# A graph network on one core: the degree sort issued beside most of the normalisation, 21 blocks gathered in the first layer, 18 gathered and 31 multiplied in the last

## The chip, the cores and the metric

The kernel runs on one core of a Trainium2 chip. The metric is the device time of one execution in microseconds (us), the median of several. Five engines work side by side, each through a queue of its own, in order: TensorE (PE in the profile, with its weight loads as PEld), VectorE (DVE), ScalarE (ACT), GpSimd (POOL) and SyncE (SP), which issues most of the plain DMAs. Indirect DMAs (gathers and scatters by a list of row numbers) are issued by POOL.

## The reference

```python
h = jnp.maximum(_layernorm(x, axis=-1), 0.0)          # x: 6250 nodes x 256
def agg(h):                                           # src, dst: 100000 edges
    return jax.ops.segment_sum(h[src], dst, num_segments=6250)
x_ = h
for l in range(3):
    h = x_ + agg(x_)
    h = relu(h @ W1s[l] + b1s[l])
    h = relu(h @ W2s[l] + b2s[l])
    x_ = h @ W3s[l] + b3s[l]
h = x_ + agg(x_)
h = relu(h @ cW1 + cb1)
h = relu(h @ cW2 + cb2)                               # 256 -> 64
out = x + (h @ cW3 + cb3)                             # 64 -> 256
```

There are four layers: three of the loop (numbered 0 to 2) and the head (3). The edges come sorted by destination. The heavy part is `x_ + agg(x_)`, a product with a sparse matrix of 6250 x 6250 counts.

## The kernel before, in words

The 6250 nodes are 49 tiles of 128 rows (`NT`). The first 36 tiles' worth of nodes (`NS`) are sorted by in-degree into 36 "s" blocks of 128 nodes, block 0 having the lowest degrees; the other 13 tiles stay as they are ("u" blocks). In each layer every block is done in one of two ways.

- *Multiplied.* The block's counts (how many edges go from each source node to each of its nodes) are built once, in layer 0, as a matrix of bytes by `build` (lines 1285 to 1341), and stored in DRAM (`mats`). In every layer they are loaded again, turned into floats by ACT (line 2118) and multiplied on PE with all the nodes' features, held in SBUF as two halves, a rounded one and the rest (`XY`). Line 2154 does that: for a panel of 3 or 4 blocks, 49 tiles x 4 matmuls of 384 or 512 columns, 196 matmuls in all. A panel is an entry `(first, number)` of `early` (layer 0), `wide` (layers 1 and 2) or `final` (layer 3), which count along the list of slots `seq`.
- *Gathered.* For each of the block's 128 nodes the c-th edge's source row is fetched by one indirect DMA of 128 rows (line 1830), two of them into one buffer, and DVE adds them up (lines 1866 to 1888). A block takes as many gathers as its cap, the highest in-degree that `reach` allows for it from the binomial law, and in layer 0 one more for the nodes' own rows. The caps of blocks 0 to 20 are 9, 10, 11, 12, 12, 12, 13, 13, 14, 14, 14, 14, 15, 15, 15, 16, 16, 16, 16, 17, 17. `nodes_of` names the gathered blocks of each layer.

Before the change layer 0 multiplies 29 blocks and gathers 20, layers 1 and 2 multiply 28 and gather 21, layer 3 multiplies 30 and gathers 19; the counts of 30 blocks are built. In gathers that is 294, 291, 291 and 257. All three small matrix products that follow (`mlp`, lines 1604 to 1750) are the same for both kinds. Results of "s" blocks are put back in their places by one indirect DMA per block from POOL (`place_rows`, lines 596 to 607).

The order on every engine is written out by hand: Python generators (`normed`, `look`, `ranking`, `listed`, `build`, `stored_later`) issue a piece of work at each `next()`, and the sequence of the calls is the order in the queues.

- `normed` (line 1022) loads x, normalises it in 25 pairs of tiles, multiplies it by the first weight and fills `XY`. After the three calls that start it, it yields 60 times, twice for each step s = 0 to 29. In step s it loads, scales pair s on ACT (1064), turns pair s-1 on PE and ACT, multiplies pair s-2 on PE (1085), copies pair s-3 out of PSUM (`out`, 1093), rounds pair s-4 on ACT (`high`, 1097), subtracts (`low`, 1102), stores pair s-5, and takes the moments of later pairs on DVE (1044).
- `look` (line 708, 24 yields) finds where each group of four nodes begins among the sorted edges: a gather of nearby edges, 17 counts on DVE (803) and ACT (807), then 16 gathers of edges by POOL (`ask`, 702), whose results DVE and ACT split and PE turns in four quarters (845 to 861). From them come the codes of the u blocks (`clT`) and of the s nodes (`cN`).
- `ranking` (line 910) counts each node's degree from `cN` and ranks the nodes (944 to 1015, PE, ACT and DVE in turn); its result is `goal`. Its last part scatters one row for each of the 36 blocks to `ranks` in DRAM (line 1017, issued at 603 by POOL).
- `listed` (line 1922) loads `ranks` back (`got`, 1925), fetches the edges of the blocks to be gathered (1931), and makes the lists of row numbers for line 1830 with DVE. On its 11th call DVE copies the node numbers out of `got` (1965); on its 14th the first list is made and layer 0's gathers begin.

Between the normalisation and layer 0's products, 28 units (`PRE`) of the counts are built, eight to a block. Then `product` (line 2126) goes tile by tile; in its layer-0 form it also calls `build` after a plan (`goals`) and `listed` at every second tile of panel 0, at every third after it. The gathers are paced over a layer by a clock of planned PE time (`work_of`, `ByNode.flow`), and each waits for the matmul issued last when it was planned (`after`).

Lines 1138 to 1203 hold the order around the change. Calling the 60 yields of `normed` h = 0 to 59: the first pieces of `look` come at h = 0 to 17, its 4 quarters at h = 25 to 41, its end after h = 51; `ranking` comes at h = 17 (its constants) and at h = 42 to 50; its 36 scatters come after h = 59, all at once. `listed` is first called in tile 0 of panel 0.

Of the kernel before, what the change touches and what calls it, by code (L numbers as in the profile page):

```python
# [9 lines left out]
F32 = mybir.dt.float32  # L10
# [6 lines left out]
OP = mybir.AluOpType  # L17
PSUM = bass.MemoryType.PSUM
DRAM = bass.MemoryType.DRAM
P = 128  # L20
# [400 lines left out]
def sorted_edges(  # L421
# [93 lines left out]
    lists_of = nodes_of[0] + [(20, 1)]  # L515
    assert sum(n for _, n in lists_of) == max(KS)
    for b0, n in lists_of:
        for b in range(b0, b0 + n):
# [17 lines left out]
    begins = const.tile([P, NS], F32, name="begins")  # L536
# [59 lines left out]
    def place_rows(key, ap, b, sb, at=None, **kw):  # L596

        at = ids if at is None else at

        if placing[0]:  # L600
            nc.gpsimd.memset(mark, 0.0)
        placing[0] = True
        got = nc.gpsimd.indirect_dma_start(  # L603
            out=ap, out_offset=bass.IndirectOffsetOnAxis(ap=at[:, b:b + 1], axis=0),
            in_=sb, in_offset=None, **kw)
        wrote(key, got, True)
# [303 lines left out]
    def ranking(pool):  # L910
# [9 lines left out]
        yield  # L920
        lag = pool.tile([P, P], F32, name="rel", bufs=1)
        nc.gpsimd.iota(lag, pattern=[[1, P]], base=0, channel_multiplier=-GD,
                       allow_small_or_imprecise_dtypes=True)
        SUB = P // GD
        row = pool.tile([P, 2], F32, name="row", bufs=1)
        nc.vector.memset(row[:, 0:1], 0.0)
        for t in range(1, GD):
            nc.vector.tensor_scalar(row[:, 1:2], place, float(SUB * t), float(P - 1), op0=OP.is_ge,
                                    op1=OP.mult)
            nc.vector.tensor_tensor(row[:, 0:1], row[:, 0:1], row[:, 1:2], OP.add)  # L930
        nc.vector.tensor_scalar(row[:, 1:2], row[:, 0:1], 0.0, None, op0=OP.is_gt)
        less_t = pool.tile([P, 2, P], BF16, name="less_t", bufs=1)
        nc.vector.tensor_scalar(less_t[:SUB, 1], lag[:SUB], float(GD - 1), -1.0, op0=OP.is_equal,
                                op1=OP.mult)
        nc.vector.tensor_scalar(lag, lag, row[:, 0:1], None, op0=OP.add)
        this = pool.tile([P, P], F32, name="f", bufs=1)
        nc.vector.tensor_scalar(this, lag, 0.0, None, op0=OP.is_equal)
        nc.vector.tensor_scalar(lag, lag, -1.0, row[:, 1:2], op0=OP.is_equal, op1=OP.mult)
        nc.vector.tensor_tensor(less_t[:, 0], this, lag, OP.subtract)
# [77 lines left out]
        yield  # L1017
        for g in range(NS):
            place_rows("ranks", ranks[:, :], g, what[:, g, :], goal)


    def normed(pool, ps_t, ps_z):
# [75 lines left out]

        def low(s):
            i0, n = pairs[s]  # L1100
            engine = nc.vector if EASY[0] <= s < EASY[1] else nc.gpsimd
            engine.tensor_tensor(XY[:, i0:i0 + n, C:], zs[s][:, :n, :],
                                    XY[:, i0:i0 + n, :C].bitcast(F32), OP.subtract)

# [31 lines left out]
            yield  # L1136

    sums = ps_g.tile([P, W], F32, name="sums")
    LOOK = (25, 27, 30, 32, 34, 36, 39, 41, 51, 53)
    RANK = tuple(range(42, 51))  # L1140
    LATER = (20, 30)

    with tc.manual_schedule():
        with tc.tile_pool(name="norm", bufs=2) as norm, tc.tile_pool(
            name="prep", bufs=2
        ) as prep, tc.tile_pool(
            name="ps_t", bufs=2, space=PSUM
        ) as ps_t, tc.tile_pool(name="ps_z", bufs=2, space=PSUM) as ps_z:
            cN = prep.tile([P, 2 * NS, GSUB], BF16, name="cN", bufs=1)
            looked = look(prep)  # L1150
            ranked = ranking(prep)
            next(looked)
            rows = normed(norm, ps_t, ps_z)
            next(rows)
# [8 lines left out]
            next(rows)  # L1163
            next(looked)
            for t, pattern, base in ((cols[:, :U * TWO], [[1, U], [2 * STEP, TWO]], NS),
                                     (cols[:, U * TWO:], [[1, NS], [2 * STEP, TWO]], 0),
                                     (lanes, [[1, P]], 0), (colf, [[1, P]], 0)):
                nc.gpsimd.iota(t, pattern=pattern, base=base, channel_multiplier=0,
                               allow_small_or_imprecise_dtypes=True)
            next(rows)  # L1170
            next(rows)
            next(looked)
            next(rows)
            turn_biases()
            nc.vector.tensor_copy(ident_r, ident)
            next(looked)
            next(rows)
            next(rows)
            for k in range(2 * NLAYER):
                next(looked)  # L1180
                next(rows)
                next(rows)
            next(looked)
            next(ranked)
            next(ranked)
            stores = stored_later(prep)
            for h, _ in enumerate(rows, 18):
                if h % 2:
                    ask(2)
                if h in LOOK:  # L1190
                    next(looked)
                if h in RANK:
                    next(ranked)
                if h in LATER:
                    next(stores)
            next(looked)
            next(ranked, None)
            assert next(ranked, 0) == 0 and next(looked, 0) == 0 and next(stores, 0) == 0

        work = ctx.enter_context(tc.tile_pool(name="work", bufs=1))  # L1200
        mat = {}
# [572 lines left out]
        class ByNode:  # L1774
# [36 lines left out]

            def send(self, upto, early=False):
                if self.l == 0:
                    upto = min(upto, self.upto[min(self.listed, len(self.upto)) - 1])
# [353 lines left out]
        def yields(slots):  # L2168
            return UNITS * slots + (slots > TOP)
# [2 lines left out]
        built, goals = [0], []  # L2172
        u0, g0 = 0, UNITS * FIRST + EARLY
        for p in range(last[0] + 1):
            u1, g1 = p * NT + NT - 2 * CH - 3, total if p == last[0] else yields(
                sum(n for _, n in early[:p + 2]))
# [7 lines left out]
        with tc.tile_pool(name="hots", bufs=1) as hots, tc.tile_pool(  # L2184
# [11 lines left out]
            while now[0] < PRE:  # L2196
                next(beside)
                next(ahead_w, None)
                built[0] += 1
                tick(layers[0])  # L2200
                layers[0].advance()
                if built[0] == UNITS * (FIRST - 1) + 3:
                    at = chunks.tile([P, 4, CH * P], U8, name="at", bufs=5)
                    nc.sync.dma_start(out=at[:, :FIRST - 1, :], in_=mats[0][:, :FIRST - 1, :CH * P])
                if built[0] == UNITS * FIRST:
                    mat[0, 0] = [(at[:, :FIRST - 1, j * P:(j + 1) * P], own_at[0][:, j, :])
                                 for j in range(CH)]
                    for _ in range(2):
                        fetch(0, 0)
# [81 lines left out]
```

## Time and profile before

| | |
|---|---|
| time, 3 runs | 1942.61 us median (1937.9 to 1942.84) |
| the profiled execution | 1944.59 us, of which the span 1942.8 us |
| mean granted PE clock | 0.977 |
| PE busy | 1814.7 us (93%), 8982 matmuls |
| POOL busy | 1396.8 us (72%) |
| ACT busy, DVE busy | 1182.1 us (61%), 898.7 us (46%) |
| product with the counts (line 2154) | 5880 matmuls, 1427.6 us |
| gathers (line 1830) | 1133, 1092.8 us |

The stages by the first and last instructions on PE: normalisation to 130.5 us, the first units of counts to 159.5, layer 0 to 673.6, layer 1 to 1098, layer 2 to 1561, layer 3 to the end. A busy share is read within its stage: POOL's instructions for indirect DMAs have some 0.3 us between them in which the profile shows no work and no wait, so that POOL at 75% is a POOL that issues without a pause.

### The profile page before, as it was taken

What the parts mean: (1) busy time and instruction counts of PE and PEld (TensorE: products, weight loads), DVE (VectorE), ACT (ScalarE), POOL (GpSimd) and SP (SyncE); (2) the same over time, 40 slices, a digit from 0 to 9 for tenths busy, and PEclk for the clock granted to TensorE, in tenths of its full rate; (3) what the DMA queues carried; (4) which work ended last, traced back from release to release, by engine and by line L of the source; (5) the groups of instructions that cost most, each with busy time, mean ns of one, the idle gap of its engine ahead of it and who ended that gap; (6) DMA issues with size and microseconds to landing.
All of it is one profiled execution on the core that took longest, in us unless ns stands there. A gap on an engine that the chain in (4) does not pass through costs nothing. (4 is left out here: it accounts for less than half of the span.)

```text
span 1942.8 us, 28380 instructions
## 1 busy us (share of the span) xinstructions
PE 1814.7 (93%) x8982; PEld 1404.6 (72%) x8982; DVE 898.7 (46%) x1892; ACT 1182.1 (61%) x2259; POOL 1396.8 (72%) x1604
## 2 busy tenths in 40 slices
PE   5777989999999989999998999999998999999896
PEld 3556777776777767777776767777776677778784
DVE  6666688777764253232334353333334343332332
ACT  4646667676766576556655475555664576666562
POOL 3557777777777577677777777777777776777775
PEclk9878999999999999999999999999999999999898
DMA  6434556666666596566565675656555776666564
GB/s 183 128 96 150 166 182 206 193 196 219 197 199 187 172 297 208 159 186 201 181 193 174 217 237 173 182 161 189 180 176 169 234 219 191 158 181 151 154 180 85
DMA packets 244986, 355.11 MB, mean 183 GB/s; under 512 B 34248, under 2 KB 199512, under 8 KB 244506
## 3 DMA queue, kind: packets, MB, share of 16 engines
q0 software_dynamic: 67792, 169.41, 30.6%
q1 hardware_dynamic: 176504, 182.73, 29.9%
q8 instruction: 72, 1.18, 0.3%
q10 hardware_dynamic: 530, 1.07, 0.2%
q14 instruction: 88, 0.72, 0.1%
HBM read 286.82 MB, written 71.78 MB: 185 GB/s over the span
## 5 line engine op out<-in xcount | busy, mean ns | idle before, releaser
L2154 PE MATMUL agg<-a,XY 128*128 128x512 f32 (+1 forms) x5880 | 1427.6, 395 | 17.8 <-ACT a L2118 14.8
L1830 POOL DMA_INDIRECT rows<-table,idxN x1113 | 1072.9, 964 | 381.2 <-PE agg L2154 162.9
L2154 PEld LDWEIGHTS agg<-a,XY 128*128 128x128 f32 x5880 | 1078.2, 190 | 246.6 <-ACT a L2118 28.5
L2118 ACT CAST a<-at 128x512 fp32r<-128x512 uint8 (+1 forms) x1463 | 846.8, 604 | 319.1 <-PE agg L2154 313.6
L1870 DVE TENSOR_TENSOR sums<-sums,rows 128x512 f32<-128x512 f32 x467 | 325.7, 697 | 552.3 <-DMA rows<-table,idxN 541.6
L1318 ACT CAST at<-bp 128x392 uint16<-128x392 f32 x213 | 103.8, 490 | 111.5 <-PE bp L1310 107.6
L1731 PE MATMUL ps<-w,h 128*128 128x256 f32 x576 | 133.5, 385 | 0.4 <-ACT h L1635 0.4
L1632 PE MATMUL ps<-h,w 128*128 128x512 f32 (+1 forms) x296 | 129.9, 581 | 3.0 <-DVE xt L1736 3.0
L1731 PEld LDWEIGHTS ps<-w,h 128*128 128x128 f32 x576 | 111.0, 193 | 17.9 <-ACT h L1635 1.1
L1256 DVE TENSOR_TENSOR lo<-lanes,pairs 128x512 bf16<-128x512 bf16 x240 | 99.7, 422 | 31.6 <-PE bp L1310 30.5
L1310 PE MATMUL bp<-hi,lo 128*128 128x98 bf16 x964 | 87.3, 215 | 24.3 <-DVE lo L1256 21.0
L1310 PEld LDWEIGHTS <-lo 128*128 128x128 bf16 x964 | 53.6, 101 | 76.0 <-DVE lo L1256 35.7
L603 POOL DMA_INDIRECT table<-zz,ids x92 | 90.7, 986 | 24.0 <-issue 16.2
L1632 PEld LDWEIGHTS ps<-h,w 128*128 128x128 f32 x296 | 55.8, 189 | 57.3 <-issue 43.9
L1736 DVE TENSOR_TENSOR zz<-ps,w 128x512 f32<-128x512 f32 x66 | 43.7, 672 | 107.5 <-PE ps L1731 105.9
L1905 ACT ACTIVATE h<-pt,bias 128x256 f32<-128x256 f32 (+1 forms) x80 | 33.1, 466 | 93.4 <-PE pt L1897 93.4
L1635 ACT ACTIVATE h<-ps,bias 128x512 f32<-128x512 f32 (+1 forms) x74 | 48.8, 678 | 50.0 <-PE ps L1632 50.0
L1256 DVE TENSOR_TENSOR hi<-hi,pairs 128x784 bf16<-128x784 bf16 x120 | 68.2, 568 | 4.2
L1866 DVE COPY sums<-rows 128x512 f32<-128x512 f32 x61 | 42.3, 694 | 57.4 <-DMA rows<-table,idxN 56.6
L603 POOL DMA_INDIRECT out_dram<-zz,ids x36 | 57.1, 1587 | 15.2 <-issue 8.5
L1256 DVE TENSOR_TENSOR hi<-cols,pairs 128x784 bf16<-128x784 bf16 x120 | 67.5, 562 | 0.9 <-ACT pairs L1244 0.9
L1416 DVE TENSOR_TENSOR XY<-turned,XY 128x512 fp32r<-128x512 f32 x54 | 37.3, 695 | 65.3 <-ACT XY L1420 65.0
(253 smaller groups left out, 987.3 us busy)
## 6 DMA issues: line engine op xcount, KB each, us to landing
at<-mat SPq DMA_DIRECT2D x126, 448.0 KB
mat<-at SPq DMA_DIRECT2D x30, 784.0 KB
at<-mat SPq DMA_DIRECT2D x62, 336.0 KB
rows<-table,idxN POOLq DMA_INDIRECT x1113
turned<-table SPq DMA_DIRECT2D x54, 256.0 KB
at<-mat SPq DMA_DIRECT2D x70, 112.0 KB
u<-own SPq DMA_DIRECT2D x61, 128.0 KB
own<-zz SPq DMA_DIRECT2D x53, 128.0 KB
```

The source lines that it names most:

```text
L603: got = nc.gpsimd.indirect_dma_start(out=ap, out_offset=bass.IndirectOffsetOnAxis(ap=at[:, b:b + 1], axis=0), in_=sb, in_offset=None, **kw)
L1256: nc.vector.tensor_tensor(o, values, which[:, :, None, :].to_broadcast(shape), op)
L1310: mm = nc.tensor.matmul(bp[:, m * HW:(m + 1) * HW], lo[:, m, :], hi[:, m, :], start=(i == 0), stop=(i == len(sets) - 1))
L1318: nc.scalar.copy(o, v)
L1632: mm = nc.tensor.matmul(ps[:, :w], weights[l][0][:, c, i * P:(i + 1) * P], h1[:, c, :w], start=(c == 0), stop=(c == KC - 1))
L1635: later(soon, lambda: nc.scalar.activation(h2[0][:, i, :w], ps[:, :w], AF.Relu, bias=b2[l][:, i:i + 1]))
L1731: mm = nc.tensor.matmul(o, h2[0][:, c, nodes], w3[:, c, :], start=(c == 0), stop=(c == KC - 1))
L1736: later(soon, lambda: nc.vector.tensor_tensor(z[:, :m, :], v, w3[:, KC:, :].to_broadcast([P, m, C]), OP.add))
L1830: got = nc.gpsimd.indirect_dma_start(out=t[:, c % 2, :], out_offset=None, in_=tables[self.l][:, :], in_offset=bass.IndirectOffsetOnAxis(ap ...
L1870: nc.vector.tensor_tensor(sums, sums, rows.rearrange("p h c -> p (h c)"), OP.add)
L2118: nc.scalar.copy(o, v)
L2154: mm = nc.tensor.matmul(agg[c][:, :w], XY[:, j, o:o + P], a[:, :w], start=(i == 0 and half == 0), stop=(i == NT - 1 and half == 1))
```

## The change

The kernel after differs in four things.

1. *Blocks.* Layer 0 gathers 21 blocks and multiplies 28 (panels of 3, 3, 3, 3, 4, 4, 4, 4 blocks in place of 3, 3, 3, 4, 4, 4, 4, 4); layer 3 gathers 18 and multiplies 31 (one panel of 3 becomes one of 4). Counts are built for 31 blocks. In gathers: 312, 291, 291 and 241. Layers 1 and 2 stay as they are.
2. *Order beside the normalisation.* The pieces of `look` and `ranking` are put at other yields t of `normed`: the counts at t = 7 and 8 all together, the 16 asks at t = 8 to 13, the four quarters at t = 12 to 21, the ranking at t = 22 to 30, and the scatters to `ranks` one at each t from 31 to 59, the last seven beside the first units of the counts. The stores of padding and of a copy of `src` move from h = 30 to t = 16, the end of `look` to t = 33 to 39.
3. *Engines.* The constants of `ranking` (`row`, `lag`, `less_t`) are made by POOL, not DVE, at t = 3. `out` is on ACT for the pairs 2 to 15 (14 pairs; before, 9 odd ones from 7 on), else on DVE. `low` is on POOL for pairs 6 to 16 (11 pairs; before, 20), else on DVE (14; before, 5).
4. *Lists.* `listed` is called in the last 10 of the 28 units ahead of layer 0, once the scatters have been issued, so that its 14th call comes at tile 6 of panel 0 (before, tile 26) and its 11th at tile 0 (before, tile 20).

```diff
-        ("u", b) for b in range(NT - 4, NT)] + [("s", 19)]
-    early = [(0, 3), (3, 3), (6, 3)] + [(b, 4) for b in range(9, 29, 4)]
+        ("u", b) for b in range(NT - 4, NT)] + [("s", 19), ("s", 18)]
+    early = [(b, 3) for b in range(0, 12, 3)] + [(b, 4) for b in range(12, 24, 4)] + [(25, 4)]
-    final = [(b, 4) for b in range(4, 24, 4)] + [(24, 3), (27, 3), (0, 4)]
+    final = [(b, 4) for b in range(4, 28, 4)] + [(28, 3), (0, 4)]
-    nodes_of = [[(16, 4), (12, 4), (8, 4), (4, 4), (1, 3), (0, 1)]] + [
+    nodes_of = [[(17, 4), (13, 4), (9, 4), (5, 4), (1, 4), (0, 1)]] + [
-        [(15, 4), (11, 4), (7, 4), (3, 4), (1, 2), (0, 1)]]
+        [(14, 4), (10, 4), (6, 4), (2, 4), (1, 1), (0, 1)]]
-    DEG, LOW, EASY = 28, 7, (9, 14)
+    DEG, LOW, EASY = 28, 7, (6, 17)
...
-        nc.vector.memset(row[:, 0:1], 0.0)
+        nc.gpsimd.memset(row[:, 0:1], 0.0)
...
         for g in range(NS):
             place_rows("ranks", ranks[:, :], g, what[:, g, :], goal)
+            yield
...
-            copy = nc.scalar.copy if s > 5 and s % 2 else nc.vector.tensor_copy
+            copy = nc.scalar.copy if 2 <= s < 16 else nc.vector.tensor_copy
...
-            engine = nc.vector if EASY[0] <= s < EASY[1] else nc.gpsimd
+            engine = nc.gpsimd if EASY[0] <= s < EASY[1] else nc.vector
...
-    LOOK = (25, 27, 30, 32, 34, 36, 39, 41, 51, 53)
-    RANK = tuple(range(42, 51))
-    LATER = (20, 30)
+    L, R, S = "look", "rank", "store"
+    BESIDE = {0: (L, "lanes"), 2: (L,), 3: ("turn", L, R), 7: (L, L), 8: (L,) * 5, 9: (4,), 11: (4,),
+              12: (L,), 13: (4, L), 14: (S,), 15: (L,), 16: (L, S), 17: (L,), 18: (L,), 20: (L,), 21: (L,),
+              33: (R, L), 36: (R, L), 39: (R, L)}
+    BESIDE.update({t: (R,) for t in range(22, 60) if t not in BESIDE})
...
-        EARLY = 4
+        EARLY, LISTED = 4, 18
...
             while now[0] < PRE:
                 next(beside)
                 next(ahead_w, None)
+                if next(ranked, 0) == 0 and built[0] >= LISTED:
+                    next(lists)
                 built[0] += 1
```

A number in `BESIDE` is a call of `ask` for so many edge gathers.

More of the change, by code (lines that the diff above doesn't have):

```diff
@@ L514, in sorted_edges @@
     starts_of, wide_of, end_of = {}, {}, 0
-    lists_of = nodes_of[0] + [(20, 1)]
+    lists_of = nodes_of[0]
     assert sum(n for _, n in lists_of) == max(KS)
@@ L535, in sorted_edges @@
     clT = const.tile([P, 3, GSUB, 2 * BUILT], BF16, name="clT")
-    begins = const.tile([P, NS], F32, name="begins")
     place = const.tile([P, 1], F32, name="place")
@@ L1149, in sorted_edges @@
             cN = prep.tile([P, 2 * NS, GSUB], BF16, name="cN", bufs=1)
+            begins = prep.tile([P, NS], F32, name="begins", bufs=1)
             looked = look(prep)
@@ L1153, in sorted_edges @@
             rows = normed(norm, ps_t, ps_z)
+            stores = stored_later(prep)
             next(rows)
@@ L1162, in sorted_edges @@
             next(rows)
[L1163 to L1195, printed above, removed]
@@ L1196, in sorted_edges @@
-            next(looked)
-            next(ranked, None)
-            assert next(ranked, 0) == 0 and next(looked, 0) == 0 and next(stores, 0) == 0
+            for t, _ in enumerate(rows):
+                for one in BESIDE.get(t, ()):
+                    if one == "lanes":
+                        for to, pattern, base in (
+                                (cols[:, :U * TWO], [[1, U], [2 * STEP, TWO]], NS),
+                                (cols[:, U * TWO:], [[1, NS], [2 * STEP, TWO]], 0),
+                                (lanes, [[1, P]], 0), (colf, [[1, P]], 0)):
+                            nc.gpsimd.iota(to, pattern=pattern, base=base, channel_multiplier=0,
+                                           allow_small_or_imprecise_dtypes=True)
+                    elif one == "turn":
+                        turn_biases()
+                        nc.vector.tensor_copy(ident_r, ident)
+                    elif isinstance(one, int):
+                        ask(one)
+                    else:
+                        next({L: looked, R: ranked, S: stores}[one])
@@ L1200, in sorted_edges @@
+            assert next(looked, 0) == 0 and next(stores, 0) == 0
         work = ctx.enter_context(tc.tile_pool(name="work", bufs=1))
@@ L1813, in send @@
                 if self.l == 0:
-                    upto = min(upto, self.upto[min(self.listed, len(self.upto)) - 1])
+                    upto = min(upto, self.upto[self.listed - 1])
                 while self.sent < min(upto, len(self.order)):
@@ L2174, in sorted_edges @@
         for p in range(last[0] + 1):
-            u1, g1 = p * NT + NT - 2 * CH - 3, total if p == last[0] else yields(
-                sum(n for _, n in early[:p + 2]))
+            u1, g1 = p * NT + NT - 2 * CH - 3, total if p == last[0] else yields(sum(early[p + 1]))
             goals.extend(g0 + (g1 - g0) * (u - u0) // (u1 - u0) for u in range(u0 + 1, u1 + 1))
```

17 lines of the change are left out of this document (8 added, 9 removed).

## The prediction

> **What bounds the kernel now.** I read first the page's busy row and then a table of windows, one row for each stage; columns are the stretch, its length, each engine's busy time (with its instructions), the granted PE clock, the DMA share and rate.
>
> ```profile
> span 1942.8 us, 28380 instructions
> 0.00:130.50 130.50, 84.20 (x524) 63.31 (x525) 82.46 (x244) 68.70 (x157) 53.36 (x107) 0.89 0.44 131
> 130.50:159.50 29.00, 22.05 (x160) 15.98 (x160) 25.23 (x62) 19.24 (x54) 24.58 (x41) 0.79 0.56 186
> 159.50:186.00 26.50, 21.21 (x140) 18.56 (x140) 14.41 (x40) 16.12 (x40) 16.31 (x31) 0.89 0.55 168
> 186.00:320.00 134.00, 123.39 (x939) 105.32 (x940) 103.29 (x290) 90.08 (x213) 103.11 (x102) 0.97 0.57 169
> 320.00:673.60 353.60, 350.86 (x1984) 255.07 (x1983) 228.21 (x531) 237.40 (x479) 264.82 (x294) 1.00 0.63 197
> 673.60:1098.00 424.40, 412.13 (x1712) 317.33 (x1712) 152.38 (x248) 248.94 (x432) 313.86 (x354) 1.00 0.64 198
> 1098.00:1561.00 463.00, 448.59 (x1864) 345.16 (x1862) 169.17 (x274) 275.76 (x480) 342.71 (x385) 1.00 0.64 195
> 1561.00:1943.00 382.00, 352.24 (x1664) 283.87 (x1664) 123.58 (x209) 225.86 (x408) 278.02 (x293) 0.96 0.61 162
> ```
>
> PE is idle for 46 us of the normalisation, 15.9 us of layer 0's first 160 us, 2.7 us of the rest of it, and 30 us of layer 3. POOL's busy column (the fifth) is three quarters from 186 us on. The timeline of POOL tells what that means: it is never free.
>
> ```profile
> 77.80 1.12 POOL L702 DMA_INDIRECT wd<-joined,starts  x1 [0.31 <-issue]
> 129.11 1.15 POOL L603 DMA_INDIRECT ranks<-what,goal  x1 [0.16 <-POOL XY L1102]
> 177.06 0.96 POOL L603 DMA_INDIRECT ranks<-what,goal  x1 [0.22 <-issue]
> 180.03 0.60 POOL L1925 DMA_DIRECT2D got<-ranks  x1 [2.00 <-DMA ranks<-what,goal]
> 185.82 1.20 POOL L1931 DMA_INDIRECT run<-padded,got  x1 [5.19 <-DMA got<-ranks]
> 196.39 1.11 POOL L1830 DMA_INDIRECT rows<-table,idxN  x1 [0.30 <-DMA run<-padded,got]
> 666.14 0.97 POOL L603 DMA_INDIRECT table<-zz,ids  x1 [2.25 <-DVE zz L1597]
> ```
>
> (Start, length, engine, line, operation, and in brackets the idle time before it with its releaser.) The 36 scatters of the ranks take from 129.1 to 178.0 us, 1.36 us each; then come 18.4 us to the first gather of layer 0 (2.0 for the scatters to land, 5.8 for `got`, eight edge fetches). From 196.4 to 667.1 us POOL puts out 294 gathers, 36 placements and some 30 edge fetches, 1.31 us each, with hardly a pause beyond the 0.3 us between any two. So layer 0 holds two full queues, PE's and POOL's, and POOL's begins 37 us after PE's (159.56 us below), because the ranks come last. The rows of PE and DVE around that:
>
> ```profile
> 53.91 1.27 DVE L933 TENSOR_SCALAR less_t<-rel 32x128 bf16<-32x128 f32 x1 [6.04 <-POOL rel L922]
> 98.80 2.66 DVE L944 TENSOR_SCALAR wd<-cN 128x1152 bf16<-128x1152 bf16 x4 [2.99 <-ACT cN L861]
> 123.73 0.20 DVE L1015 SCALAR_TENSOR_TENSOR goal<-where 128x36 int32<-128x36 int32 x1
> 185.07 0.19 DVE L1965 COPY ids<-got 128x36 int32<-128x36 int32 x1 [5.74 <-DMA got<-ranks]
> 118.79 3.04 PE L1085 MATMUL bp<-w,ht 128*128 128x256 f32 x12
> 130.51 0.81 PE L1310 MATMUL bp<-hi,lo 128*128 128x98 bf16 x8 [2.82 <-POOL mark L601]
> 159.56 1.62 PE L2154 MATMUL agg<-a,XY 128*128 128x384 f32 x4 [1.13 <-DVE a L2116]
> 186.19 0.51 PE L1310 MATMUL bp<-hi,lo 128*128 128x98 bf16 x4 [5.42 <-DVE lo L1256]
> ```
>
> **The change: up to the asks.** Up to t = 3 the order is the same. Then the counts, which were spread over six steps, come in one burst, and so do the edge gathers:
>
> ```profile
> 23.36 0.95 DVE L792 TENSOR_SCALAR near<-near_i,low 98x1408 f32<-98x1408 int32 x1
> L803 DVE TENSOR_SCALAR_CACHE_REDUCE wd<-near 98x448 bf16<-98x448 f32 x11 | 6.7, 612 | 0.2
> L702 POOL DMA_INDIRECT wd<-joined,starts x16 | 15.9, 994 | 9.4 <-issue 3.3 <-PE bp L1085 3.1 <-DVE row L930 2.6
> L1102 POOL TENSOR_TENSOR XY<-zs,XY 128x512 fp32r<-128x512 f32 x19 | 24.4, 1282 | 47.0 <-ACT XY L1097 47.0
> ```
>
> From 24.3 us eleven counts (6.7 us), two or three copies of the norm and the small steps to `starts` end at about 35 us. PE's queue holds the small product for `begins` behind them, and pairs 2 and on behind that: PE stands for some 5 us there. Sixteen asks of 0.99 + 0.3 us go out from 35 to 56 us (before, the last ended at 78.9); no `low` of POOL lies among them any more. The fourth quarter's edges land 2 to 3 us later, and the codes are done at about 62 to 64 us, where before only the first quarter was. DVE carries pairs 6 to 14's moments and lows 0 to 5 in the same stretch and is full: the asks can't bring it below that.
>
> The stall of 6.04 us (DVE behind POOL's `lag`) goes, since POOL makes the constants itself, before the asks.
>
> **The ranking and its scatters.** It took 25.1 us (98.80 to 123.9) with 4.5 steps of the norm between its parts, and has 4.5 steps again: from 64 to 89 us, bounds 84 and 95. Then 36 scatters at 1.36 us and six `low`s at 1.28 us are 56.7 us of POOL: the end is at 146 us, in place of 178. POOL was idle in over half of the norm, so nothing else is pushed; lows 11 to 16 wait up to 5 us more, which the five `zs` buffers cover (if not, ACT's `out` five pairs later waits). The 18.4 us to the first gather stay: it comes at 164.5 us, 32 us earlier, bounds 158 and 172. It needs tile 6 of panel 0 to have been reached, which it has.
>
> **The norm's end.** Pair by pair PE's products went, free and beside look:
>
> ```profile
> 61.83 1.89 PE L1085 MATMUL bp<-w,ht 128*128 128x256 f32 x8
> 66.42 1.99 PE L1085 MATMUL bp<-w,ht 128*128 128x256 f32 x8
> 76.50 1.89 PE L1085 MATMUL bp<-w,ht 128*128 128x256 f32 x8
> 85.93 1.92 PE L1085 MATMUL bp<-w,ht 128*128 128x256 f32 x8
> ```
>
> That is two pairs in 4.6 us and three in 9.4, or 2.3 and 3.1 each. At 64 us PE is at pair 8 (before, 10), at the ranking's end at pair 13; eleven more at 2.75 end at 120 us, against 121.8. But the 8.7 us from there to 130.51, in which DVE did the end of the ranking and of look, shrink to about 4 (the last copy and subtraction): counts start at 124 us, 6.5 earlier, and layer 0's tile 0 at 153, bounds 145 and 158. There `ids` waits for `got`, which lands 7 us after the last scatter, at 153: a stall of 0 to 3 us in place of 5.42, with the counts' compares behind it on DVE and PE behind those. Then PE is 11.5 us early.
>
> **Layer 0.** One block less is 196 matmuls of 384 columns for 512. The chain of waits has both, undisturbed:
>
> ```profile
> 1189.05 22.40 PE agg L2154 x96
> 1845.67 14.08 PE agg L2154 x80
> L1310 PE MATMUL bp<-hi,lo 128*128 128x98 bf16 x964 | 87.3, 215 | 24.3 <-DVE lo L1256 21.0
> ```
>
> 233.3 less 176.0 ns, times 196, is 11.2 us. One more block of counts is 32 matmuls at 87.3/964 us, 2.9 us at most, half of it perhaps. PE alone would thus end layer 0 at 11.5 + 11.2 - 2 = 21 us earlier. POOL has 18 gathers and an edge fetch more, 19 x 1.28 = 24 us, against a start 32 us earlier: 8 us earlier, and up to 12 if the few us of slack it had are used up. The later queue decides; I take 10.
>
> **Layers 1 and 2.** The same counts, the same gathers: 0, with 2 us either way.
>
> **Layer 3.** Here PE waits for rows that came late. In the waits of 1562 to 1943 us (who, for whom: sum, times, longest):
>
> ```profile
> DVE sums L1870 <- DMA rows<-table,idxN: 167.7, 65, 12.1
> PE ps L1646 <- DVE zz L1715: 10.5, 3, 7.5
> PE pt L1897 <- DVE u L1884: 5.7, 2, 3.4
> ```
>
> The page's group of gathers (busy, mean ns of one, then the idle before them):
>
> ```profile
> L1830 POOL DMA_INDIRECT rows<-table,idxN x1113 | 1072.9, 964 | 381.2 <-PE agg L2154 162.9
> ```
>
> POOL loses 16 gathers at 0.96 + 0.30 us, 20 us; PE gains 11.2. PE's waits of 16.2 us go as POOL draws ahead, for PE and POOL part by 31 us over the layer: 16.2 - 11.2 = 5.0 us earlier. If a third of the waits stay (POOL still blocks itself with placements in fours), it is nothing, and with two thirds 6 us later. I take 4.5.
>
> **The sum.** 10 + 4.5 = 14.5 us off the profiled 1944.59 us (span 1942.8), or 1930.1; that execution stands 2.0 us above the median, so the forecast in the median's terms is 1928.1 us.
>
> **The rivals.**
>
> *PE's queue decides layer 0.* If rank and scatters come early enough (first gather at 155) or POOL's step is nearer 1.25 than 1.31, layer 0 gains all of PE's 21 us, and with layer 3's 4.5 it is 1917 us. For it: PE was idle only 2.7 us in layer 0's second part though POOL was full. Against: POOL was full.
>
> *The gain is eaten ahead of layer 0.* The scatters now run beside the norm, not alone beside the counts:
>
> ```profile
> L603 POOL DMA_INDIRECT ranks<-what,goal x36: 964/972/1337, 129.1 to 177.1; - x36
> ```
>
> Minimum, median and maximum in ns: were each at the maximum, 36 x 0.365 = 13 us would be added, layer 0's gain would be gone, and the time 1941 us. A burst that holds the norm back as much would do the same. By the Trainium skill, SBUF — State Buffer, section "Who interferes with whom", VectorE in its two-port modes locks GpSimd out of SBUF while GpSimd writes the descriptors of a DMA, and copies and tensor_scalar are named among these; it would speak for this rival, since DVE's work for the norm lies beside the scatters now. This trace doesn't bear it out: the asks, which ran beside the norm already, took 994 ns on average.
>
> *Slower: the 21st block has no room.* If the ranking comes little earlier than before, say because DVE, full to 64 us, drags the codes to 85 us and the ranking's end to 110, POOL's 57 us end at 167 and the first gather comes at 185, 11 us earlier, against 24 us more work: layer 0 ends 13 us later, layer 3 gives back 4.5, and the time is 1951 us; with two thirds of layer 3's waits kept as well (6 later in place of 4.5 earlier), 1962. The turn lies at a first gather at 172 us (196.4 - 24). For it: DVE, ACT and PE depend on each other in order through the whole norm, and DVE is 82 of 130 us busy. Against: the ranking is issued 20 yields earlier, a third of the norm.
>
> **How the numbers follow.** A measurement of this kernel can tell about 0.3%, 5.8 us, from no change. Forecast 0.5; PE-decided 0.2; eaten 0.18; slower 0.12. Faster by over 5.8 us are the first two and a few hundredths of the third: 0.72. The same: most of the third and part of the last: 0.18. Slower: 0.10. The first's own range is 1920 to 1936 (bounds of the first gather, 158 to 172, and layer 3's 0 to 5). To hold 8 in 10, the range goes down to 1912, which takes in the PE-decided case with a norm 4 us shorter still, and up to 1943, which takes in the eaten one.
>
> **What would show it.** In the profile after: the last ask before 60 us; `goal` at 84 to 95; the last scatter to `ranks` at 140 to 153; the first gather at 158 to 172; the first product at 145 to 158, with at most 3 us of waiting for `got`; layer 0's 4 placements at its end, and layer 1's first tile, 8 to 12 us earlier than 673.6; layers 1 and 2 at 424 and 463 us; layer 3 with under 5 us of PE waiting for rows. The forecast is wrong where the first gather comes after 172 us, or PE stands in layer 0 for over 15 us after 320 us, or layer 3 is no shorter than 382 us.

## The result

The changed kernel takes 1933.16 us (median of 6 runs, 1928.43 to 1935.49), the kernel before 1942.72 us beside it (6 runs, 1937.9 to 1943.63): 0.9948 of it, with a 95% interval of 0.9936 to 0.996. The forecast was 1928.1 us, a ratio of 0.9925. The profiled execution took 1929.31 us, 3.9 us under its median, where the one of before stood 2.0 us above its own; so the two profiles differ by 15.3 us, the medians by 9.6. What is said below of stages comes from the profiles. The first eight of the experiments below ran on two other chips, on which the kernel before takes 2229 to 2230 us; each ratio stands against the kernel before on the same chip.

### The profile page after: what moved, and what is told of

It reads as the page before. It is cut to its first block, busy times and chain, and to the rows that moved or that the text cites. A ratio compares the mean times of both kernels' runs of the same rounds, so it can differ in the third digit from the quotient of the medians.

```text
span 1927.5 us, 28422 instructions
## 1 busy us (share of the span) xinstructions
PE 1798.9 (93%) x9026; PEld 1412.2 (73%) x9026; DVE 905.6 (47%) x1905; ACT 1185.6 (62%) x2273; POOL 1398.4 (73%) x1610
## 5 line engine op out<-in xcount | busy, mean ns | idle before, releaser
L2138 PE MATMUL agg<-a,XY 128*128 128x512 f32 (+1 forms) x5880 | 1405.3, 391 | 18.8 <-ACT a L2102 14.8
```

The costliest lines, as they stand in the source:

```text
L2138: mm = nc.tensor.matmul(agg[c][:, :w], XY[:, j, o:o + P], a[:, :w], start=(i == 0 and half == 0), stop=(i == NT - 1 and half == 1))
```

## The profile after

First the busy row of the page, then the table of windows with the edges at the changed kernel's own stages (columns: stretch, its length, busy time with instructions of PE, PEld, DVE, ACT and POOL, the granted clock, DMA share and rate).

```profile
span 1927.5 us, 28422 instructions
```

```profile
0.00:124.20 124.20, 82.70 (x524) 64.75 (x525) 83.19 (x235) 72.45 (x162) 69.60 (x150) 0.88 0.46 138
124.20:154.20 30.00, 21.54 (x160) 15.47 (x160) 26.01 (x67) 20.02 (x57) 20.97 (x35) 0.82 0.55 184
154.20:180.00 25.80, 25.68 (x171) 22.51 (x172) 21.51 (x68) 18.58 (x46) 18.61 (x20) 0.88 0.72 230
180.00:320.00 140.00, 129.15 (x993) 108.85 (x992) 104.43 (x294) 92.34 (x218) 107.52 (x107) 0.96 0.58 175
320.00:672.60 352.60, 338.92 (x1951) 250.98 (x1950) 231.80 (x528) 228.56 (x477) 262.86 (x286) 0.98 0.61 194
672.60:1096.00 423.40, 409.50 (x1714) 321.93 (x1713) 152.44 (x248) 248.18 (x433) 314.78 (x356) 0.98 0.64 198
1096.00:1554.00 458.00, 440.01 (x1862) 345.59 (x1860) 168.85 (x273) 274.60 (x480) 338.90 (x382) 0.99 0.64 196
1554.00:1928.00 374.00, 351.35 (x1658) 282.08 (x1658) 117.42 (x199) 230.91 (x407) 265.20 (x279) 0.98 0.60 162
```

The norm is shorter (124.2 us to the counts, 130.5 before), the first products lie denser. But layer 0's second part, in which PE was idle for 2.7 us before, now has 13.7 us of idle PE, and its length is the same: 352.6 and 353.6 us. Layers 1 and 2, which the change leaves as they are, went from 887.4 to 881.4 us together: PE's busy time fell there from 860.7 to 849.5 us, its idle time rose from 26.7 to 31.9. Layer 3 went from 382 to 374 us between like edges, though it multiplies one block more.

The timeline of POOL (start, length, line, operation, idle time before with its releaser) shows the gathers' queue from the first rank to layer 0's last placement:

```profile
90.82 1.03 POOL L602 DMA_INDIRECT ranks<-what,goal  x1 [3.63 <-DVE goal L1013]
144.01 1.10 POOL L602 DMA_INDIRECT ranks<-what,goal  x1 [0.22 <-issue]
147.16 0.60 POOL L1909 DMA_DIRECT2D got<-ranks  x1 [2.05 <-DMA ranks<-what,goal]
162.72 0.94 POOL L1814 DMA_INDIRECT rows<-table,idxN  x1 [1.70 <-PE bp L1294]
652.57 0.94 POOL L1814 DMA_INDIRECT rows<-table,ids  x1 [0.30 <-issue]
657.68 0.97 POOL L602 DMA_INDIRECT table<-zz,ids  x1 [0.21 <-issue]
665.11 0.96 POOL L602 DMA_INDIRECT table<-zz,ids  x1 [6.37 <-DVE zz L1581]
```

The first gather comes 33.7 us earlier than before (196.39), the last placement ends at 666.1 us, 1.0 us earlier than before (666.14 + 0.97 = 667.1). Counted along this timeline, POOL issues 374 operations from the first gather to the last one, in 490.8 us; before it was 352 in 458.5. The 22 more are the block's 18 gathers, an edge fetch, and three placements that now go out ahead of the last gather instead of behind it. From the last gather to the last placement it is 12.6 us, where it was 12.2, though four placements stand there now and eight before: 6.37 us of it POOL waits for DVE's `zz`. So the account of layer 0 is -33.7 + 32.3 + 0.4 = -1.0 us.

PE's rows at the end of the norm, and its waits in layer 0's second part (who, for whom: sum, times, longest):

```profile
33.91 0.64 PE L831 MATMUL ps<-ident,f 98*128 98x36 f32 x2 [7.54 <-DVE f L830]
118.22 2.76 PE L1084 MATMUL bp<-w,ht 128*128 128x256 f32 x12
124.22 0.65 PE L1294 MATMUL bp<-hi,lo 128*128 128x98 bf16 x8 [3.25 <-POOL mark L600]
154.25 1.62 PE L2138 MATMUL agg<-a,XY 128*128 128x384 f32 x4 [1.81 <-DVE a L2100]
```

```profile
PE pt L1546 <- DVE u L1872: 4.0, 1, 4.0
PE bp L1294 <- DVE lo L1240: 3.9, 4, 2.8
PE pt L1881 <- DVE u L1872: 3.5, 1, 3.5
```

Tile 0 is at 154.25 us, 5.3 earlier than before, and there is no stall for `got`. `u` is the sum of a block's gathered rows: PE stands where POOL's rows come late, and before this was 0.2 us.

In layer 3 the waits of PE, and its products by shape:

```profile
PE pt L1881 <- DVE u L1868: 5.6, 1, 5.6
PE agg L2138 <- ACT a L2102: 4.7, 5, 1.4
PE ps L1673 <- ACT h L1638: 2.3, 3, 1.2
PE ps L1630 <- DVE zz L1699: 1.8, 1, 1.8
```

```profile
L2138 PE MATMUL agg<-a,XY 128*128 128x512 f32 x1304 | 307.0, 393 | 4.7 <-ACT a L2102 4.7
L2138 PE MATMUL agg<-a,XY 128*128 128x384 f32 x196 | 35.8, 338 | 0.0
```

The wait for `zz` fell from 10.5 to 1.8 us. PE's busy time did not grow by the 11.2 us that the wider panel should add: the 512-wide product takes 393 ns on average where it took 400 in the same layer before. A part of that is not the waits' doing. The same 52 products in one run without a pause, at the full granted clock in both profiles, first before, then after:

```profile
1570.60 12.38 PE L2154 MATMUL agg<-a,XY 128*128 128x512 f32 x52
```

```profile
1563.40 12.08 PE L2138 MATMUL agg<-a,XY 128*128 128x512 f32 x52
```

That is 238 and 232 ns for each, with the same instructions, and it is so in layers 1 to 3; in layer 0, where the runs of products are short, eight of them take some 262 ns each in both. It goes with the program and not with the chip: all kernels below that gather 21 blocks in layer 0 take 232 ns (last_as_before 234), all with 20 take 238, and three of the chips had kernels of both kinds. This is where PE's busy time went in layers 1 and 2. Which part of layer 0's new lines brings it about was not tested.

## The experiments

Theory A: in the changed kernel POOL's queue sets the end of layer 0, and the 21st block's gathers use up what the earlier ranks bring; layer 3's gain is POOL's relief. Rival B: layer 0 goes by PE and the pacing of the plan. Rival C: layer 3's shorter time is the granted clock of one execution. "Last placement" is layer 0's last row of `table<-zz,ids` in POOL's timeline; "layer 3" is from the last placement of layer 2 to the last placement into the output, 408.1 us in the profile of before and 398.4 in that of after.

### Order and blocks taken apart

**order_alone**, the changed kernel with the blocks of before:

```diff
-    nodes_of = [[(17, 4), (13, 4), (9, 4), (5, 4), (1, 4), (0, 1)]] + [
+    nodes_of = [[(16, 4), (12, 4), (8, 4), (4, 4), (1, 3), (0, 1)]] + [
...
-        [(14, 4), (10, 4), (6, 4), (2, 4), (1, 1), (0, 1)]]
+        [(15, 4), (11, 4), (7, 4), (3, 4), (1, 2), (0, 1)]]
```

with `seq`, `early`, `final`, `lists_of` and the cap in `send` as before.

> The new order ahead of layer 0 with the blocks of before (layer 0 gathers 20 and multiplies 29, layer 3 gathers 19 and multiplies 30). Theory A (in the changed kernel POOL's gathers set the end of layer 0, the earlier first gather only pays for the 21st block, and layer 3's gain comes from POOL's relief): with 20 blocks POOL is no longer last, PE is, and it starts some 5 us earlier and has no 5.4 us stall for the ranks: layer 0 ends 7 to 11 us before 673.6 us, layer 3 lasts 421 us as before, the time is about 1934 us (0.995 to 0.9965 of before). Rival B (layer 0 goes by PE's work and the pacing of the plan, and the 21st block is what made the layer's end 1 us earlier): layer 0 ends no earlier than 673 us, and the time is 1940 to 1943 us.

**first_as_before** undoes only layer 0's line (with `early`, `lists_of` and the cap), **last_as_before** only layer 3's (with `seq` and `final`), **blocks_alone** puts both new lines into the kernel before.

> The changed kernel with layer 0 as before (20 gathered, 29 multiplied), layer 3 as changed (18 and 31). Theory A: layer 0 ends 7 to 11 us earlier than before and layer 3 keeps its 8 to 10 us, so the time is about 1925 us, 8 us below the changed kernel's 1933. Rival B: the layer loses 11 us of PE work saved by the 21st block and the time is 1938 to 1944 us.

> The changed kernel with layer 3 as before (19 gathered, 30 multiplied), layer 0 as changed (21 and 28). Theory A: layer 0 ends at 673 us, layer 3 lasts 420 to 422 us, and the time is 1941 to 1943 us, about that of before. Rival C (layer 3's shorter time in the one profile is the granted clock of that execution, not the blocks): 1933 to 1936 us.

> The blocks of the changed kernel (layer 0: 21 gathered, 28 multiplied; layer 3: 18 and 31) in the order of before, with the small tile of the lists' beginnings in the pool of the norm, as in the changed kernel, to make room. Theory A: the first gather stays at 196 us, POOL has some 24 us more work behind it of which a few us were slack, so layer 0 ends 17 to 24 us after 673.6 us; layer 3 gives back 8 to 10; the time is 1950 to 1958 us. Rival B: PE's 196 matmuls of less width count and layer 0 ends at 665 to 675 us, and with layer 3's gain the time is 1925 to 1935 us.

These four ran on one chip, where the kernel before took 2229.23 us (18 runs), and four more on another, at 2230.03 us (11 runs). Of those, **first_as_before_2** and **order_alone_2** are repeats, **after_again** is the changed kernel, and **no_own_row** leaves the node's own row out of layer 0's sums, one gather less for each block:

```diff
-                    k, r = len(self.order), caps[b + i] + (l == 0)
+                    k, r = len(self.order), caps[b + i]
```

> The changed kernel itself once more, beside the others on one chip, since the first four kernels ran on a chip where the kernel before took 2229 us in place of 1943 and engines stood without a releaser in the trace. On a chip like the first it should be 0.9936 to 0.996 of before. On a chip like that of the four it is the missing corner: if the parts add up there (order alone 0.983, layer 0's block 1.1% more, layer 3's block 0.3% more), 0.997.

> The changed kernel with one gather less for each of layer 0's 21 gathered blocks: the node's own row is left out of the sums of layer 0, so POOL has 21 gathers (21 x 1.28 = 27 us) less there, DVE some ten additions less, and PE the same work. Theory A (POOL sets layer 0's end): layer 0 ends when PE is done, 8 to 13 us earlier than the changed kernel's 672.6 us, and the time falls by as much, to about 1923 us or 0.990 of before. Rival B (PE and the plan's pacing set it): within 3 us of the changed kernel, 1930 to 1936 us.

> The kernel of first_as_before once more (new order; layer 0 gathers 20 and multiplies 29 as before; layer 3 gathers 18 and multiplies 31), for a chip like the first one. Theory A: layer 0 ends 7 to 11 us before 672.6 us, layer 3 keeps its gain: about 1925 us, 0.991 of before. Rival B: 11 us of PE work are back and the time is 1938 to 1944 us. On a slow chip like that of the first four: 0.986 of before again.

> The kernel of order_alone once more (new order, blocks of before in both layers), for a chip like the first one. Theory A: layer 0 ends 7 to 11 us before 672.6 us, layer 3 takes 421 us: about 1934 us, 0.9955 of before, and 8 to 10 us above first_as_before_2. Rival C (layer 3's blocks are worth nothing): as first_as_before_2. On a slow chip like that of the first four: 0.983 of before again.

| kernel | gathered in layers 0, 3 | first gather | last placement ends | layer 3 | median us | ratio to before, 95% |
|---|---|---|---|---|---|---|
| blocks_alone | 21, 18 | 213.1 | 794.8 | 433.8 | 2235.93 | 1.0034 (1.0018 to 1.0051) |
| last_as_before | 21, 19 | 186.6 | 764.4 | 451.6 | 2213.82 | 0.9941 (0.992 to 0.9963) |
| first_as_before | 20, 18 | 196.1 | 771.9 | 436.4 | 2196.8 | 0.9862 (0.9837 to 0.9886) |
| first_as_before_2 | 20, 18 | 196.6 | 772.6 | 433.2 | 2194.14 | 0.9836 (0.9805 to 0.9867) |
| order_alone | 20, 19 | 186.1 | 745.5 | 448.6 | 2185.69 | 0.9831 (0.9803 to 0.9858) |
| order_alone_2 | 20, 19 | 181.1 | 736.4 | 448.4 | 2185.84 | 0.9809 (0.9781 to 0.9837) |
| after_again | 21, 18 | 182.5 | 769.9 | 437.1 | 2206.65 | 0.9904 (0.9867 to 0.9941) |
| no_own_row | 21 less a gather each, 18 | 184.9 | 745.9 | 431.1 | 2177.76 | 0.9784 (0.9751 to 0.9818) |

None of the times in us of the expectations could be met there. Of the ratios, after_again was to be at 0.997 if order and blocks simply added up; it is at 0.9904, so there they don't. What the table says beside that:

Layer 3 is settled. With 18 gathered blocks it takes 431 to 437 us in five runs, with 19 it takes 448 to 452 in three. On the chips like the first it splits the same way: 398.1 to 400.5 us with 18 (after, first_as_before_3, two_rows_less), 408.1 to 410.8 with 19 (before, before_again, order_alone_3). Rival C is refuted.

Layer 0's end follows the gathers. The rows behind that, the last placements of after_again and of no_own_row:

```profile
768.91 0.97 POOL L602 DMA_INDIRECT table<-zz,ids  x1 [7.71 <-DVE zz L1581]
```

```profile
744.97 0.97 POOL L602 DMA_INDIRECT table<-zz,ids  x1 [1.73 <-DVE zz L1581]
```

21 gathers left out, some 27 us of POOL, end the layer 24 us earlier, with PE's work the same; rival B allowed 3. And blocks_alone ends it 30 us after last_as_before on the same chip, with the same blocks in layer 0 and the first gather 27 us later. But POOL's queue is not full on these chips: between the first and the last gather of layer 0 its pauses of over 0.5 us add up to some 115 us in after_again and 120 in no_own_row, against 1 us in the changed kernel's first profile. So these runs show that the end hangs on the number and the start of the gathers, not that a full queue sets it.

What did not fit is first_as_before: by A it should end layer 0 with order_alone, and on both chips it ends it 26 to 36 us later. 10 and 15.5 us of that stand at the first gather already. These chips add something of their own (last section), and it differs between kernels whose instructions up to there are the same. So the price of the 21st block had to be read on a chip without it.

### On a chip like the first

**before_again** is the kernel before, **order_alone_3** order_alone; **two_rows_less** has `caps[b + i] - (l == 0)` in the line of no_own_row.

> The kernel before, for its trace on a chip like those of the first eight runs (2230 us). There the last placement of layer 0 stood at 770 us in the changed kernel, at 795 with the new blocks in the old order, at 736 to 746 with the old blocks in the new order. Theory A (order and 21st block add up: the order brings the gathers forward, the block uses it up): 780 us here, so that the order is worth 35 to 45 us, the block 15 to 25. Rival D (the new order is worth little by itself, and the old blocks are fast in any order): 740 to 760 us. Layer 3, from the last placement of layer 2 to the last one into the output: 448 us, as in the two others with 19 gathered blocks there.

> As no_own_row, but with two gathers less for each of layer 0's 21 blocks (the node's own row and the last slot of its list are left out of the sums): 42 gathers, 54 us of POOL, less than the changed kernel. Theory A: the first 21 gathers took 24 us off the end of layer 0 (770 to 746 us); the next 21 take off much less, since PE's queue is then last: layer 0's last placement at 730 to 746 us, the time at 2160 to 2180 us (0.97 to 0.98 of before). Rival E (POOL's queue sets the end by its length alone, PE has 50 us of room): 718 to 724 us, and 2150 us.

> order_alone in one more look, beside before_again on one chip: layer 0's last placement 35 to 45 us ahead of before_again's by theory A, under 15 us by rival D. If the chip is like the first one (1943 us): 7 to 11 us ahead by theory A, and the time 1934 us.

This chip took 1941.66 us for the kernel before (7 runs), so the question of before_again (rival D on the slower chips) stays open; as a second look at the kernel before it gave 1946.55 us, the last placement at 667.8 and layer 3 at 409.7 us. two_rows_less took 1906.92 us (4 runs), 0.9824 of before (0.98 to 0.9848); order_alone_3 1937.79 us in its one look. Windows of 320 to 650 us, in order: before, after, order_alone_3, two_rows_less.

```profile
320.00:650.00 330.00, 327.82 (x1889) 238.35 (x1888) 221.61 (x519) 224.17 (x453) 252.66 (x275) 1.00 0.64 200
```

```profile
320.00:650.00 330.00, 320.71 (x1882) 237.63 (x1881) 226.91 (x519) 219.55 (x460) 254.73 (x274) 0.98 0.63 200
```

```profile
320.00:650.00 330.00, 328.16 (x1839) 238.51 (x1831) 215.85 (x484) 223.77 (x451) 238.32 (x263) 1.00 0.63 195
```

```profile
320.00:650.00 330.00, 325.43 (x1906) 240.56 (x1906) 218.19 (x498) 222.49 (x465) 223.69 (x250) 1.00 0.61 193
```

The fifth busy column is POOL's. Its 275 and 274 operations in before and after leave 77 and 75 us idle, 0.28 us for each, and that is the pause between any two; order_alone_3 leaves 0.35 and two_rows_less 0.43 for each, so there POOL has time over. Its timeline from the first gather to the last says it more plainly: pauses of over 0.5 us add up to 2 us in before and 1 us in after, but to 31 us in order_alone_3 and 56 us in two_rows_less. PE (first column) is idle for 2.2 us in before, 9.3 in after, 1.8 in order_alone_3 and 4.6 in two_rows_less, whose layer 0 ends inside the window. With 20 blocks in the new order, or with gathers left out, PE is nearly full and POOL is not. The layer's ends in these two:

```profile
660.51 0.97 POOL L602 DMA_INDIRECT table<-zz,ids  x1 [3.10 <-DVE zz L1581]
```

```profile
644.36 0.96 POOL L602 DMA_INDIRECT table<-zz,ids  x1 [3.02 <-DVE zz L1581]
```

order_alone_3 ends layer 0 at 661.5 us, 6.3 us ahead of before_again; A had 7 to 11, and under 15 was rival D's mark, so this run alone doesn't tell them apart. Its norm ended later than the changed kernel's: the first product of layer 0 stands at 161.47 us, against 154.25.

two_rows_less ends it at 645.3 us, 20.8 earlier than the changed kernel, and its whole time is 22.2 us less in the profiles (1907.1 and 1929.31, on two chips). The numbers expected were those of the slower chips, but the reading holds: 54 us of POOL work left out bring 21 us, because PE is last then. PE alone ends layer 0 at 645 us, 22 us earlier than before; POOL takes 21 of these 22 back.

### Is the 21st block worth it?

**first_as_before_3** is first_as_before on one more chip, where the kernel before took 1940.7 us (11 runs).

> The kernel of first_as_before a third time (new order, layer 0 gathers 20 and multiplies 29, layer 3 gathers 18 and multiplies 31), for a chip on which the kernel before takes 1942 us: is the 21st block in layer 0 worth anything once the order is new? Theory A, with what order_alone_3 showed (layer 0's last placement at 661.5 us, PE last): one more block's counts, 3 to 5 us of PE, puts it at 664 to 667 us, where the changed kernel has 666; layer 3 keeps its 10 us; the time is 1929 to 1935 us, 0.993 to 0.9965 of before, as the changed kernel. Rival F (the 21st block saves PE's 11 us in layer 0 after all): layer 0's last placement at 670 to 677 us and the time 1938 to 1945 us. On a chip like those of the first eight runs: 0.984 to 0.986 of before again.

It took 1926.92 us (6 runs), 0.9921 of before (0.99 to 0.9942), a little under what A expected, since the layer's end came earlier than the 664 to 667 us that it gave.

```profile
320.00:650.00 330.00, 327.42 (x1860) 237.32 (x1859) 217.38 (x492) 223.72 (x453) 237.86 (x263) 1.00 0.61 193
```

```profile
658.96 0.97 POOL L602 DMA_INDIRECT table<-zz,ids  x1 [3.10 <-DVE zz L1581]
```

PE is full, POOL is not, and layer 0 ends at 659.9 us, 6.2 us ahead of the changed kernel, with a first gather at about the same time (163.8 and 162.7). Rival F (670 to 677) is refuted: the 21st block costs layer 0 some 6 us, as far as two executions on two chips can tell. Layer 3 takes 398.1 us, as in the changed kernel (398.4). So new order, 20 gathered in the first layer and 18 in the last is the best version of these: 0.9921 against 0.9948, on different chips, with intervals that just overlap. The one block's counts more are paid for: first_as_before_3 needs 504.6 us from its first product of layer 0 (155.29 us) to the layer's end, order_alone_3, which builds them for one block less, 500.0 us. The 4.6 us lie within the 3 to 5 expected; first_as_before_3 ended the layer earlier only because its first product came 6.2 us earlier.

## Why the prediction was right, and where it wasn't

The time came out in the range and near the forecast, but that the sum of the profiles was met so closely (14.5 us forecast, 15.3 measured) is luck: its two terms were off in opposite directions, and a stage that was set at 0 gave 6.1 us. Layer 0 gave 1.0 us where 10 were taken, layer 3 gave 9.7 where 4.5 were. From layer 0's last placement to layer 2's it is 857.3 us before and 851.2 after. The end behind the last placement took 1.5 us more: -1.0 - 6.1 - 9.7 + 1.5 = -15.3.

**Layers 1 and 2: not foreseen.** "The same counts, the same gathers: 0" took it that the same instructions take the same time. Their products went from 238 to 232 ns each, which brought PE's busy time down by 11.2 us; 5.2 of these came back as idle time. The new order seems to be worth some 3 us there as well: before_again has 857.1 us, order_alone_3 and first_as_before_3, with the new order and products of 238 ns, 853.6 and 854.4, and two_rows_less, with both, 849.4. Each is one execution.

**Up to the asks, ranking, scatters: right.** The last ask ends at 56.05 us (56 forecast), the ranking at 90.8 (89 forecast), the scatters at 145.1 (146), the first gather is at 162.72 (164.5). PE stood 7.54 us behind the burst of counts, where some 5 were forecast.

**The norm's end: right.** Counts at 124.2 (124), tile 0 at 154.25 (153), no stall.

**Layer 0: the mechanism right, the size wrong.** "The later queue decides" holds: two_rows_less measured 22 us for the 21 us by which PE alone was to end it earlier. What failed is the step "18 gathers and an edge fetch more, 19 x 1.28 = 24 us". Between the first and the last gather there were 22 operations more, 28.7 us at the 1.303 us that one took before, because three placements had moved ahead of the last gather; and 3.6 us came from POOL's mean step, 1.312 us over 374 operations. That mean isn't steady: before_again, the same program as before, has 1.314. And moving the placements up saved nothing behind, since the last block's way from gather to placement (12.2 and 12.6 us) is a chain of its own. The slack that was to make 8 into 12 wasn't there either. So the sign that the prediction named, layer 1's first tile 8 to 12 us earlier than 673.6, was missed: it is at 672.6.

**Layer 3: the mechanism right, too small.** The waits for `zz` and `u` that were to vanish fell from 16.2 to 7.4 us, not to 0, and are over the 5 us that the prediction named as its mark. But the 11.2 us of product work did not show: PE's busy time in the layer is 351.35 us, against 352.24. The sum lacked two things. One is the product's step: 6 ns less for each of some 1400 products is 8 us, an estimate. The other is the clock, 0.98 of full speed over the layer for 0.96. Behind before's longest wait, which ended at 1831.6 us, stands this row:

```profile
1831.60:1838.40 6.80, 6.76 (x27) 5.82 (x28) 3.38 (x6) 2.41 (x6) 5.27 (x6) 0.62 0.40 113
```

PE worked there at 0.62 of its clock, in finer windows at 0.50 up to 1836.7 us and at 1.00 behind that, so the wait cost some 2.6 us (0.38 of 6.8) more than its own 7.5. The Trainium skill gives the rule in TensorE: Matmul & The Clock Gate, section "What's actually happening": an idle window puts PE on half its clock until it has been busy for a window again. This trace agrees. Over the layer, in windows of 1 us, PE's clock was at half for some 28 us before and 17 after, which is worth at most 5.6 us. The forecast took the wait as the whole price.

first_as_before_3 has the same blocks in layer 3 and the product of 238 ns:

```profile
1551.00:1924.70 373.70, 358.35 (x1658) 282.41 (x1658) 117.13 (x199) 231.62 (x407) 263.67 (x278) 0.98 0.59 162
```

```profile
PE pt L1881 <- DVE u L1868: 1.9, 1, 1.9
```

There the mechanism shows almost as forecast: the waits fell from 16.2 to 1.9 us, and PE's busy time rose, by 6.1 us, with the clock better than before as in the changed kernel. The stage takes 373.7 us, as long as in the changed kernel (374), whose PE is busy for 7 us less and idle for 7 us more. So the faster product did not shorten the layer: PE's work alone doesn't set its length. The 16 gathers less are what remains, but no run varied them by themselves.

**The rivals.** PE didn't decide layer 0 in the changed kernel (two_rows_less shows what it would have been). The gain wasn't eaten ahead of layer 0: the 36 scatters, now beside the norm, have a median of 985 ns and a longest of 1399, for 972 and 1337, and a mean of 1041 for 1063. The rule of the Trainium skill, SBUF — State Buffer, section "Who interferes with whom", isn't borne out by them. The slower case named the right cost, the block that has no room, but its condition (a first gather after 172 us) didn't hold; blocks_alone, with the first gather at 213 us on its chip, is that case, and it was 0.3% slower than before.

Not settled: how much of the 9.6 us between the medians is layer 3's and how much layers 1 and 2's, since the medians have no stages; and why the same product takes 232 ns in one program and 238 in the other.

## What to carry to other kernels

A queue that starts earlier by a time t brings t less everything that is put into it after that, and operations that are moved ahead of its last one count too; what then follows the last operation is a chain that doesn't shrink with the queue. Which of two full queues is last is best asked by leaving out work of one of them: with 42 gathers less the layer lost 21 us of the 54, and that named POOL, PE's floor and the room between them at once. A wait of PE can cost its own length and a stretch of lower clock behind it (2.6 us behind 7.5 here), so removing it can be worth more than it is long. And before a stage's gain is put down to the change made in it, compare one instruction in runs of equal number in both profiles: here the most frequent one had become 2.5% faster in layers that nobody had touched.

## What was not expected of the hardware

On the two chips of the first eight runs the kernel before takes 15% longer, and the changed kernel 14%. A part of that is waits of PE that the first chip doesn't show. PE's waits in after_again, over the whole span:

```profile
PE agg L2138 <- issue: 85.6, 105, 2.4
PE bp L1294 <- DVE lo L1240: 28.9, 19, 5.3
PE bp L1294 <- issue: 28.0, 14, 6.3
```

"issue" means that the trace shows nothing that PE waited for; in after there is no such row among PE's nine longest waits. PE, DVE and ACT often stand together, and where they stand depends on the program: in first_as_before, on both chips, they hardly moved from 127 to 155 us, while POOL's scatters went on at their usual pace. Rows of first_as_before_2:

```profile
131.42 3.43 PE L1084 MATMUL bp<-w,ht 128*128 128x256 f32 x8 [4.20 <-ACT ht L1075]
138.51 0.69 DVE L1092 COPY zs<-bp 128x512 f32<-128x512 f32 x1 [9.96 <-remote]
142.50 2.08 PE L1084 MATMUL bp<-w,ht 128*128 128x256 f32 x4 [7.64 <-issue]
155.33 0.69 DVE L1092 COPY zs<-bp 128x512 f32<-128x512 f32 x1 [15.53 <-remote]
```

The changed kernel, whose instructions are the same on every engine up to layer 0, has no pause of that length on the second of these chips. The DMA queues moved 2 GB/s in most of that stretch, and one packet of instructions landed at 137 us and the next at 157, so the arrival of instructions doesn't explain the two resumptions between them. The cause stays open. It also leaves open why first_as_before lost 26 to 36 us of layer 0 to order_alone there and none on the last chip.
